# A state-space vision block on one core: the first pair of images is scanned by rows first, and half of its projections are made in slots beside the scans

## The chip, the core and the metric

The kernel runs as one program on one core of one Trainium2 chip. A core has five engines that run beside each other and meet at semaphores: PE (matrix products), DVE (vector work), ACT (functions of one operand), POOL (a second, slower vector engine) and SP, which here does nothing but issue DMAs, one after the other. The metric is the device time of one launch in microseconds (us). Instructions of one engine start in the order in which the program lists them; an instruction that waits holds up everything behind it on its engine. For SP that means that one DMA that waits for its data holds up all later DMAs.

## What is computed

Eight images of 96 channels and 64 x 64 pixels go through three layers: a state-space block with a convolutional branch, linear attention, and a feed-forward layer in reduced precision. The change bears on the first of them. Cut to what matters:

```python
def ss2d(x, ...):                                  # x: (8, 64, 64, 96), normalized
    xi, z = split(einsum('bhwc,oc->bhwo', x, in_proj_w), 2)
    xi = silu(conv2d(xi, conv_w, conv_b, groups=192))          # depthwise 3x3
    x_flat = xi.reshape(b, 192, L)                             # rows,    L = 4096
    x_wh   = transpose(xi, (0, 1, 3, 2)).reshape(b, 192, L)    # columns
    xs = [x_flat, x_wh, flip(x_flat), flip(x_wh)]              # k = 0, 1, 2, 3
    dts, Bs, Cs = split(einsum('bkdl,kcd->bkcl', xs, x_proj_w), [6, 22])
    dts = einsum('bkrl,kdr->bkdl', dts, dt_w)
    for each step l:                                           # 192 channels x 16 states
        h = exp(softplus(dts + bias) * A) * h + delta * u * B
        y = sum_n h * C                                        # plus D * u
    y = out_y[0] + flip(out_y[2]) + turned(out_y[1]) + turned(flip(out_y[3]))
    return einsum('bhwd,cd->bhwc', layer_norm(y) * silu(z), out_proj_w)

x1  = x * skip_scale + ss2d(layer_norm(x))
cb  = conv2d(gelu(conv2d(layer_norm(x1), w1)), w2)             # then channel attention
out = x1 * skip_scale2 + cb * sigmoid(...)
```

Each image is scanned four times: along its rows forwards (k = 0) and backwards (k = 2), and along its columns forwards (k = 1) and backwards (k = 3).

## The kernel before

**Pairs and scans.** The eight images are taken in four pairs p. The 192 channels of two images make three tiles T of 128 partitions: image 0's first 128 channels, image 1's first 128, and the last 64 of both. For each pair there are four sweeps k. A sweep runs over four chunks of 1024 steps (ci) and the three tiles, which is 12 jobs, and a job over 16 units of 8 channels x 16 states; so a sweep has 192 units and the kernel 3072. For one unit PE spreads delta * u over the states (`pu`, function spread), DVE multiplies by B (`pb`) and scans (`hc`, function scan), POOL multiplies by C, and PE adds the states up (`yp`, function total). ACT makes the decays (`da`). The sweeps come in the order (1, 3, 0, 2) for each pair, so columns first. A later sweep adds to what an earlier one of the same kind left: k = 3 to k = 1 (`prev`), k = 2 to k = 0 (`prev`) and, through `yet`, to the columns' sum.

**Slots and lanes.** All other work of phase_b is written as Python generators, called lanes, and handed out while the program is written. There are two slots to a pair of units, so 16 to a job and 3072 to the scans. In each slot every lane may put down its next few instructions. A lane that needs PSUM calls `take`, which gives out one of two banks (`pg`, `yp`) if the budget for PE and ACT isn't used up; the budget grows by RATE (1.4 for PE, 1.6 for ACT) with each slot. Nothing is decided at run time: the order on each engine is fixed when the program is built (class InOrder ties it down).

**The lanes.** before_scans(p) makes what pair p's scans need: norms (layer norm, stored in a padded image ua_d), convs (nine-tap convolutions on PE with weights wmain and wmix, the gate z with wz, then silu, and the projection of the rows), turn (POOL turns rows into columns) and at last the projection of the columns. It starts at the beginning of pair p-1's sweeps and works on one image after the other. columns(p) adds the two column sweeps, turned back, to D * u. It is put in during the k = 0 sweep of the same pair. after_scans(p) runs gate (layer norm, silu gate, output projection) and then starts two lanes rest (the convolutional branch, attention and feed-forward) for pair p during pair p+1. For the last pair, last_gate and last_rest do a part of this at the end, and a tail after the scans does what is left.

**The first pair.** No scans lie in front of it. So phase_a makes its whole first stage before the scans: for each of the two images one load of 1.5 MB, statistics on DVE (L108, L110), normalization on DVE (xn, L136 and L137) and on POOL (xt, L138 and L139), transposes (L145, L157), then eight blocks of two nine-tap convolutions and one gate product (L184, L193), POOL copies to columns (L203, L206), stores, and 8 row and 8 column projections (L221, L222, L225, stored by L227). The convolution weights are multiplied together on DVE from taps loaded one by one (projections, L64 to L66).

After phase_a come the loads of phase_b's weights (function load, L403), the feed-forward weights' casts, and zeros for the borders of the padded images: a zeroed tile is written over ua_d, u_d and g_d in 18 DMAs (L479). Then SP issues the first job's loads: `st` and `du`, `bm` (B for 32 x 4 rows), the store and reload of delta (`dl`), `cm`.

```python
        jobs = [
            (p, k, ci, T) for p in range(NP) for k in (1, 3, 0, 2)
            for ci in range(NCH) for T in (0, 2, 1)
        ]
```

Of the kernel before, what the change touches and what calls it, by code (L numbers as in the profile page):

```python
# [71 lines left out]
def phase_a(tc, a, proj, xi_d, zs_d, inp_d, xd_d):  # L72
# [3 lines left out]
    wmain, wmix, wz, xwa, xwb, convb = proj  # L76
    with ExitStack() as ctx:
        cp = ctx.enter_context(tc.tile_pool(name="a_const", bufs=1))
        xp = ctx.enter_context(tc.tile_pool(name="a_x", bufs=2))
        sp = ctx.enter_context(tc.tile_pool(name="a_small", bufs=2))  # L80
        op = ctx.enter_context(tc.tile_pool(name="a_out", bufs=2))
        bp = ctx.enter_context(tc.tile_pool(name="a_big", bufs=1))
        ps = ctx.enter_context(tc.tile_pool(name="a_ps", bufs=6, space=PSUM))
        pst = ctx.enter_context(tc.tile_pool(name="a_pst", bufs=1, space=PSUM))

        ident = cp.tile([128, 128], F32, name="ident")
# [3 lines left out]
        vec = cp.tile([C, 10], F32, name="vec")  # L90
        nc.sync.dma_start(vec, a["vec96"])
# [3 lines left out]
        for i in range(2):  # L95
            pad = cp.tile([C, H + 2, W + 2], F32, name=f"pad{i}")
            nc.gpsimd.memset(pad, 0.0)
            pads.append(pad)

        for b in range(2):  # L100
            p, half = divmod(b, 2)
            xt = xp.tile([128, G, C], F32, name="xt")
            nc.sync.dma_start(xt, a["x"][b].rearrange("(g p c) -> p g c", p=128, c=C))

            st = sp.tile([128, G, 6], F32, name="st")
            tmv = sp.tile([128, G, 2], F32, name="tmv")
            for g in range(G):
                nc.vector.bn_stats(st[:, g, :], xt[:, g, :])  # L108
            for g in range(G):
                nc.vector.bn_aggr(tmv[:, g, :], st[:, g, :])  # L110
            tm, tv = tmv[:, :, 0], tmv[:, :, 1]
            gps = pst.tile([128, 2, G], F32, name="gps")
            nc.tensor.matmul(gps[:, 0, :], mean128, tm, start=True, stop=True)
            gm = sp.tile([128, G], F32, name="gm")
            nc.vector.tensor_copy(gm, gps[:, 0, :])
            q = sp.tile([128, G], F32, name="q")
# [3 lines left out]
            nc.tensor.matmul(gps[:, 1, :], mean128, q, start=True, stop=True)  # L120
            r = sp.tile([128, G], F32, name="r")
            nc.scalar.activation(r, gps[:, 1, :], AF.Sqrt, bias=eps)
            nc.vector.reciprocal(r, r)

            s = sp.tile([128, G], F32, name="s")
# [6 lines left out]
            def wide(v):  # L132
                return v.unsqueeze(2).to_broadcast([128, G, C])

            xn = xp.tile([128, G, C], F32, name="xn")
# [3 lines left out]
            nc.gpsimd.tensor_mul(xt, xt, wide(r))  # L139

            pad = pads[b % 2]
            for j in range(8):
                tp = ps.tile([128, 512], F32, name="ps")
                for g in range(4):
                    nc.tensor.transpose(  # L145
                        tp[0:C, g * 128 : g * 128 + 128], xn[:, 4 * j + g, :], ident
                    )
                nc.scalar.activation(
                    pad[:, 1 + 8 * j : 9 + 8 * j, 1 : W + 1],
                    tp[0:C, :].rearrange("p (h w) -> p h w", w=W),  # L150
                    AF.Identity,
                    bias=vec[:, LN1B : LN1B + 1],
                    scale=vec[:, LN1G : LN1G + 1],
                )
                ti = ps.tile([128, 512], F32, name="ps")
                for g in range(4):
                    nc.tensor.transpose(  # L157
                        ti[0:C, g * 128 : g * 128 + 128], xt[:, 4 * j + g, :], ident
                    )
                if j % 4 == 0:  # L160
                    inp = op.tile([C, 2048], F32, name="inp")
                nc.vector.tensor_copy(inp[:, (j % 4) * 512 : (j % 4) * 512 + 512], ti[0:C, :])
                if j % 4 == 3:
                    nc.sync.dma_start(inp_d[b][:, (j - 3) * 512 : (j + 1) * 512], inp)


            rows = slice(64 * half, 64 * half + 64)
            xis = bp.tile([128, L], F32, name="xis")
            mix = bp.tile([128, L], F32, name="mix")
            xiw = bp.tile([128, L], F32, name="xiw")  # L170
            mixw = bp.tile([64, L], F32, name="mixw")

            def flipped(t, at):
                return t.rearrange("p (w h) -> p h w", h=H)[:, at.start // W : at.stop // W, :]

            for j in range(8):
                if j % 4 == 0:
                    zss = op.tile([128, 2048], F32, name="zss")
                at = slice(j * 512, j * 512 + 512)
# [20 lines left out]
                nc.scalar.activation(zss[:, (j % 4) * 512 : (j % 4) * 512 + 512], pz, AF.Silu)  # L200
                if j % 4 == 3:
                    cols = slice((j - 3) * 512, (j + 1) * 512)
                    nc.gpsimd.tensor_copy(  # L203
                        flipped(xiw, cols), xis[:, cols].rearrange("p (h w) -> p h w", w=W)
                    )
                    nc.gpsimd.tensor_copy(  # L206
                        flipped(mixw, cols), mix[0:64, cols].rearrange("p (h w) -> p h w", w=W)
                    )
                    nc.sync.dma_start(xi_d[0][p][half][:, cols], xis[:, cols])
                    nc.sync.dma_start(xi_d[0][p][2][rows, cols], mix[0:64, cols])  # L210
                    nc.sync.dma_start(zs_d[p][half][:, cols], zss)
                    nc.sync.dma_start(zs_d[p][2][rows, cols], mix[64:128, cols])
            nc.sync.dma_start(xi_d[1][p][half], xiw)
            nc.sync.dma_start(xi_d[1][p][2][rows, :], mixw)
            for o, main, rest in ((0, xis, mix), (1, xiw, mixw)):
                for j in range(8):
                    if j % 2 == 0:
                        xd = op.tile([PR, 1024], F32, name="xd")
                    at = slice(j * 512, j * 512 + 512)
                    px = ps.tile([128, 512], F32, name="ps")  # L220
                    nc.tensor.matmul(px[0:PR, :], xwa[:, o, :], main[:, at], start=True, stop=False)  # L221
                    nc.tensor.matmul(  # L222
                        px[0:PR, :], xwb[0:64, o, :], rest[0:64, at], start=False, stop=True
                    )
                    nc.vector.tensor_copy(xd[:, (j % 2) * 512 : (j % 2) * 512 + 512], px[0:PR, :])  # L225
                    if j % 2 == 1:
                        nc.sync.dma_start(xd_d[o][b][:, (j - 1) * 512 : (j + 1) * 512], xd)  # L227
# [88 lines left out]
def wait(n):  # L316
    for _ in range(n):
        yield
# [63 lines left out]

def phase_b(
    tc, a, proj, xi_d, xd_d, dl_d, ya_d, ys_d, y_d, zs_d, inp_d, x1_d, ua_d, u_d, g_d, cb_d, tn_d,
# [7 lines left out]
    with ExitStack() as ctx:  # L392
        cp = ctx.enter_context(tc.tile_pool(name="b_const", bufs=1))
        inner = ExitStack()
        bcp = inner.enter_context(tc.tile_pool(name="b_bc", bufs=4))
        wp = inner.enter_context(tc.tile_pool(name="b_w", bufs=2))
        hp = inner.enter_context(tc.tile_pool(name="b_h", bufs=8))
        gp = inner.enter_context(tc.tile_pool(name="b_bg", bufs=1))
        psc = inner.enter_context(tc.tile_pool(name="b_ps", bufs=1, space=PSUM))
# [6 lines left out]
        def unit(i):  # L406

            return gp.tile([128, 8 * PH if i in (0, 1, 6, 7) else 512], F32, name=f"u{i}")
# [20 lines left out]
        wmain, wmix, wz, xwa, xwb, convb = proj  # L429
# [27 lines left out]
        w1f, w2f = unit(0)[0:C, 0:HID], unit(1)[:, 0 : 3 * C]  # L457
        nc.sync.dma_start(w1f, a["w1T"])
        nc.sync.dma_start(w2f, a["w2T"].rearrange("p i c -> p (i c)"))
        b1r = load("b1", [128, 3])  # L460
        nc.vector.tensor_copy(w1q, w1f, saturate=False)
        nc.vector.tensor_copy(w2q.rearrange("p i c -> p (i c)"), w2f, saturate=False)
        nc.vector.tensor_copy(b1q, b1r, saturate=False)
        nc.vector.tensor_copy(b2q, vec[:, B2 : B2 + 1], saturate=False)
        nc.vector.tensor_copy(b1f, b1q)
        nc.vector.tensor_copy(b2f, b2q)
# [6 lines left out]
        zeros = gp.tile([128, 2048], F32, name="big0")  # L473
        nc.gpsimd.memset(zeros, 0.0)
        for i in range(2):
            for t, n in ((ua_d[i], C), (u_d[i], C), (g_d[i], 32)):
                for c0 in range(0, PH * PH, 2048):
                    c1 = min(c0 + 2048, PH * PH)
                    nc.sync.dma_start(t[:, c0:c1], zeros[0:n, 0 : c1 - c0])  # L479
# [13 lines left out]
            (p, k, ci, T) for p in range(NP) for k in (1, 3, 0, 2)  # L493
# [4 lines left out]
        turned = set()  # L498
# [52 lines left out]
        def columns(p):  # L551

            yield from slots.take_big(0, 1)
# [1320 lines left out]
```

## Time and profile before

| | |
|---|---|
| runs of the kernel | 11,445.26 us median of 3 (11,439.81 to 11,451.60) |
| the profiled execution: its own time, its span | 11,441.71 us, 11,439.9 us |
| mean granted PE clock | 0.814 of full speed |
| busy: DVE, POOL, PE, ACT | 92%, 79%, 71%, 57% of the span |
| DMA | 1,818 MB, mean 159 GB/s, one hardware queue |
| one unit: pb, hc on DVE | 1.216 us, 2.27 to 2.33 us |
| one unit: hc on POOL | 2.358 us |

The profile is of one execution. Busy time of an engine is the sum of its instructions; idle time costs only where the engine is the bound. A row names the tile that an instruction writes and those that it reads, as in "hc<-hc,cm". Line L242 is the helper through which all of phase_b's ordered instructions go, so there rows are told apart by tiles and not by lines. The chain of waits follows the last instruction back to what released it, and so on to the start; "issue" in it is time in which nothing that the profile shows was waited for. The windows give each engine's busy time in a stretch, and the granted clock there.

### The profile page before, as it was taken

Reading aid. Unit: us, or ns where it says so; the run is one execution under the profiler, and the core shown is the slowest. Engines: PE = TensorE matmul, PEld = TensorE weight load, DVE = VectorE, ACT = ScalarE, POOL = GpSimd, SP = SyncE. Lnnn points to the kernel's source line nnn. Section 1 sums busy time; section 2 is a strip of 40 time slices with the busy share of each in tenths; the row PEclk is TensorE's granted clock in tenths of the full one; section 3 lists DMA queues with packets and bytes.
Section 4 is the critical chain, followed back from the end, with each engine's and each line's share of the span. In section 5 each row is a group of like instructions: output and inputs, shape, how many; then the busy total and the mean of one; then the engine's idle time right before and its main releaser. Section 6 shows DMA issues by size and latency. Waiting matters only on the chain.

```text
span 11439.9 us, 127234 instructions
## 1 busy us (share of the span) xinstructions
PE 8086.3 (71%) x39524; PEld 3206.6 (28%) x39524; DVE 10551.6 (92%) x6613; ACT 6548.1 (57%) x9092; POOL 8995.2 (79%) x6573
## 2 busy tenths in 40 slices
PE   7658677465577876687767887677757677665778
PEld 3223222122222332233222333233322233222223
DVE  2399999999999999899999999999999999999984
ACT  1265555444466666666556666666646656774554
POOL 1387778977788779978889778987979889997870
PEclk9778778677788887788878888788878887777889
DMA  2444445554455555645545556644645555553551
GB/s 67 145 128 151 145 142 175 176 179 142 141 159 159 158 177 186 198 151 183 187 149 165 155 164 187 199 158 154 212 146 166 160 164 189 178 170 126 173 159 37
DMA packets 876693, 1818.33 MB, mean 159 GB/s; under 512 B 234669, under 2 KB 413614, under 8 KB 867246
## 3 DMA queue, kind: packets, MB, share of 16 engines
q1 hardware_dynamic: 876014, 1810.20, 50.4%
q8 instruction: 313, 5.13, 0.2%
q14 instruction: 366, 3.00, 0.1%
HBM read 1389.34 MB, written 420.42 MB: 158 GB/s over the span
## 4 chain that ended last, share of the span: by engine, by line
PE 38%; issue 26%; DVE 17%; POOL 7%; ACT 6%; DMA 4%; SPq 1%; DVEq 0%; POOLq 0%; ACTq 0%
PE pu L242 13%; PE yp L242 13%; DVE hc L242 10%; PE pg L242 8%; DVE pb L242 6%; POOL hc L242 5%; ACT u L242 2%; PE ps L184 2%; ACT da L242 2%; PE t L242 2%; DMA bm<-xd 1%; POOL u L242 1%; ACT L242 1%; DMA xd<-xd 0%; POOL turn L242 0%
## 5 line engine op out<-in xcount | busy, mean ns | idle before, releaser
L242 POOL TENSOR_TENSOR hc<-hc,cm 128x1024 f32<-128x1024 f32 x3072 | 7226.8, 2358 | 754.3 <-DVE hc L242 516.1
L242 DVE TENSOR_TENSOR_SCAN hc<-da,carry,pb 128x1024 f32<-128x1024 f32 x2304 | 5272.2, 2330 | 61.7 <-ACT da L242 59.0
L242 PE MATMUL pu<-du,c_sel 128*128 128x512 f32 x3072 | 2477.0, 953 | 2282.1 <-DVE pb L242 2278.2
L242 DVE TENSOR_TENSOR pb<-pu,bm 128x1024 f32<-128x1024 f32 x3072 | 3595.4, 1216 | 237.4 <-PE pu L242 193.4
L242 ACT ACTIVATE da<-dl,c_alog 128x1024 f32<-128x1024 f32 x3072 | 3356.1, 1140 | 132.9 <-DVE hc L242 111.9
L242 ACT COPY y<-yp 128x256 f32<-128x256 f32 x768 | 284.1, 370 | 2828.0 <-PE yp L242 2728.9
L242 PEld LDWEIGHTS pu<-du,c_sel 128*128 128x128 f32 x3072 | 807.6, 287 | 3571.2 <-DVE pb L242 2793.3
L242 DVE TENSOR_TENSOR_SCAN hc<-da,pb 128x1024 f32<-128x1024 f32 x768 | 1710.8, 2269 | 44.4 <-ACT da L242 44.1
L242 PE MATMUL yp<-hc,c_add 128*32 128x256 f32 x24576 | 1645.3, 413 | 63.7 <-ACT dls L242 40.1
L242 PEld LDWEIGHTS yp<-hc,c_add 128*32 128x32 f32 x24576 | 765.5, 119 | 1218.4 <-issue 630.3
L242 POOL COPY carry<-hc 128x1 f32<-128x1 f32 x2304 | 422.0, 183 | 768.4 <-DVE hc L242 750.7
L242 ACT ACT_TABLE_LOAD x554 | 710.8, 1283 | 80.9 <-DMA du<-xi 54.3
L242 POOL TENSOR_TENSOR u<-u,u 96x512 f32<-96x512 f32 (+1 forms) x426 | 537.7, 1269 | 100.2 <-ACT u L242 95.8
L242 POOL TENSOR_TENSOR du<-du,dls 128x1024 f32<-128x1024 f32 x192 | 453.3, 2361 | 141.7 <-ACT dls L242 140.6
L242 ACT COPY u<-pg 128x512 f32<-128x512 f32 (+5 forms) x345 | 189.0, 548 | 454.9 <-PE pg L242 448.6
L242 PE MATMUL pg<-ain,wmain 96*128 96x512 f32 x864 | 422.2, 634 | 21.5 <-ACT u L242 19.4
L242 PE MATMUL pg<-ain,wmix 96*128 96x512 f32 x864 | 402.2, 609 | 30.0 <-ACT u L242 30.0
L242 ACT COPY u<-yp 128x512 f32<-128x512 f32 (+4 forms) x351 | 188.2, 536 | 388.0 <-PE yp L242 361.9
L242 PE MATMUL yp<-prev,ident 128*128 128x256 f32 x768 | 311.0, 496 | 12.2 <-ACT dls L242 7.1
L242 PEld LDWEIGHTS yp<-prev,ident 128*128 128x128 f32 x768 | 213.4, 279 | 344.4 <-issue 273.9
L242 PE MATMUL pg<-st,dtw 12*128 12x512 f32 x384 | 220.3, 654 | 78.5 <-DMA dtw<-in_dtw 45.0
L242 PE MATMUL yp<-u,c_centres 128*128 128x512 f32 (+3 forms) x578 | 266.3, 647 | 8.1 <-ACT u L242 4.0
(335 smaller groups left out, 7061.9 us busy)
## 6 DMA issues: line engine op xcount, KB each, us to landing
dl<-dl SPq DMA_DIRECT2D x768, 512.0 KB
bm<-xd SPq DMA_DIRECT2D x512, 512.0 KB
cm<-xd SPq DMA_DIRECT2D x512, 512.0 KB
du<-xi SPq DMA_DIRECT2D x192, 512.0 KB
dl<-dls SPq DMA_DIRECT2D x192, 512.0 KB
ya<-y SPq DMA_DIRECT2D x384, 128.0 KB
prev<-ya SPq DMA_DIRECT2D x384, 128.0 KB
xi<-u SPq DMA_DIRECT2D x120, 256.0 KB
```

What stands on the lines that cost most here:

```text
L184: nc.tensor.matmul(pc.rearrange("p (h w) -> p h w", w=W), w[:, t, :], pad[:, 8 * j + dy : 8 * j + dy + 8, dx : dx + W], start=(t == 0), st ...
L242: op(*args, **kw)
```

## The change

1. Pair 0's sweeps come in the order (0, 2, 1, 3): rows first. The other pairs keep theirs.
2. phase_a loads and normalizes the two images in eight pieces of 7 to 9 groups of 128 pixels. Only the first half of each image is convolved there, in four chunks of 1024 pixels, with row projections and no column work. Both normalized images are written, padding included, to ua_d. It comes after the opening of phase_b's weight pool and ahead of the scans' pools, and calls projections itself after the first piece.
3. before_scans runs for p = 0 as well, from the first job: convolutions for j = 4 to 7 of both images, in two lanes at a time, then turn and the column projections, then fill. For p = 1 it starts when that has ended, also with two convs lanes, and two norms lanes. For p = 2 and 3 it is as it was.
4. fill is new: in slots it casts the feed-forward weights and writes the zeros of u_d and g_d. The zeros for ua_d go away.
5. columns(0) runs during pair 1, ahead of pair 0's gate. It reads the rows' result and adds it to the columns; pair 0's k = 2 sweep doesn't load `yet`.
6. A scan job's first loads are only put down once its data are there (the set `there`); if they aren't, 16 slots at a time are handed out with no scan in them.
7. RATE rises to 1.5 and 1.7. The last gate's start is tied to the slot at which a chunk is left, and not to a fixed number.

The diff, cut to its core:

```diff
@@ phase_a
+        pieces = [
+            (b, g0, g1) for at in (((0, 9), (9, 17)), ((17, 25), (25, 32)))
+            for b in range(2) for g0, g1 in at
+        ]
+        for b, g0, g1 in pieces:
+            xt = xp.tile([128, 9, C], F32, name="xt")
+            nc.sync.dma_start(
+                xt[:, 0 : g1 - g0, :],
+                a["x"][b].rearrange("(g p c) -> p g c", p=128, c=C)[:, g0:g1, :],
+            )
...
+        got = normalize(*pieces[0])
+        proj = wmain, wmix, wz, xwa, xwb, convb = projections(tc, a, pp)
+        for n, (b, g0, g1) in enumerate(pieces):
+            transposes(b, g0, g1, *got)
+            if n + 1 < len(pieces):
+                got = normalize(*pieces[n + 1])
+            if n < 4:
+                chunk(b, n % 2)
+            elif n % 2:
+                nc.sync.dma_start(ua_d[b], pads[b].rearrange("c h w -> c (h w)"))
@@ Slots
-    RATE, CAP = (1.4, 1.6), (2.2, 2.2)
+    RATE, CAP = (1.5, 1.7), (2.2, 2.2)
@@ phase_b
-        zeros = gp.tile([128, 2048], F32, name="big0")
-        nc.gpsimd.memset(zeros, 0.0)
-        for i in range(2):
-            for t, n in ((ua_d[i], C), (u_d[i], C), (g_d[i], 32)):
-                for c0 in range(0, PH * PH, 2048):
-                    c1 = min(c0 + 2048, PH * PH)
-                    nc.sync.dma_start(t[:, c0:c1], zeros[0:n, 0 : c1 - c0])
...
-            (p, k, ci, T) for p in range(NP) for k in (1, 3, 0, 2)
+            (p, k, ci, T) for p in range(NP) for k in ((1, 3, 0, 2) if p else (0, 2, 1, 3))
@@ columns
+            to = ys_d[0] if p else y_d
...
+                    if p == 0:
+                        yr = unit(c % 2)[:, 0:512]
+                        nc.sync.dma_start(yr, y_d[p][T][:, at])
...
+                    if yr is not None:
+                        ge.tensor_add(t, t, yr)
@@ after_scans
+            if p == 0:
+                yield from columns(p)
+            while resting:
+                yield
             yield from gate(p, range(8))
@@ new
+        def fill():
...
+            se.copy(w1q, w1f, saturate=False)
...
+            ge.memset(big, 0.0)
+            yield from wait(2)
+            for i in range(2):
+                for t, n in ((u_d[i], C), (g_d[i], 32)):
+                    for c0 in range(0, PH * PH, 2048):
+                        c1 = min(c0 + 2048, PH * PH)
+                        nc.sync.dma_start(t[:, c0:c1], big[0:n, 0 : c1 - c0])
+                        yield
@@ before_scans
+            js = range(0 if p else 4, 8)
+            at_once = p < 2
...
+            if at_once:
+                for half in range(2):
+                    slots.lanes.append(convs(2 * p + half))
+                    if p:
+                        slots.lanes.append(norms(2 * p + half))
+                while len(there_all) < 2:
+                    yield
...
+            there.update((p, 1, c) for c in range(NCH))
+            if p == 0:
+                yield from fill()
+                slots.lanes.append(before_scans(1))
@@ the loop over units
+                        if p == 0 and T == 0:
+                            slots.lanes.append(before_scans(0))
+                        if p > 0 and T == 2:
+                            slots.lanes.append(columns(p))
...
+                        while (p, k % 2, c) not in there:
+                            for _ in range(16):
+                                slots.run()
+                        slots.first = steps(job)
```

## The prediction

> **What bounds the kernel now.** I read the page's busy shares first (DVE 92%, no other engine over 79%), then the windows, to see where the other 8% of DVE lies, then the chain of waits there.
>
> Windows at the start; columns are the stretch, its length, busy time (instructions) of PE, weight loads, DVE, ACT and POOL, the granted clock, the DMA share and GB/s:
>
> ```profile
> core 0: us, PE busy (x) PEld busy (x) DVE busy (x) ACT busy (x) POOL busy (x), PEclk, DMA share, GB/s
> ...
> 100.00:200.00 100.00, 100.00 (x235) 43.98 (x234) 0.00 (x0) 11.83 (x18) 7.42 (x2) 1.00 0.10 32
> ...
> 400.00:500.00 100.00, 32.40 (x55) 8.79 (x58) 35.74 (x38) 20.35 (x20) 22.53 (x17) 0.58 0.70 218
> 500.00:600.00 100.00, 52.72 (x312) 20.05 (x304) 100.00 (x62) 52.20 (x92) 80.69 (x66) 0.72 0.38 117
> ```
>
> The front is PE-bound with DVE idle; from 500 us on DVE is full. The first scan starts at 475.81 us, the last ends near 11,100, and the tail takes 340 us. The front's chain, in order of time (start, length, what):
>
> ```profile
> 79.01 15.46 PE ps L184 x36
> ...
> 364.69 15.47 PE ps L184 x36
> 380.92 3.70 POOL mixw L206
> 386.14 14.01 DMA xd<-xd
> ...
> 430.36 2.11 SPq L479
> ...
> 462.95 6.29 DMA dl<-dls
> 471.06 5.82 DMA du<-xi
> ```
>
> To be seen: 16 blocks of two nine-tap convolutions, two strings of projections that wait for xd stores, then 26 us in which SP issues border zeros (L479, 427.8 to 454.3), then the load-up of the first scan.
>
> The scans, by sweep (192 units each): pair 0's four, then pair 1's third:
>
> ```profile
> 475.80:1129.60 653.80, 437.60 (x2092) 165.59 (x2092) 644.59 (x384) 368.14 (x564) 511.40 (x364) 0.78 0.44 138
> 1129.60:1799.40 669.80, 482.34 (x2260) 197.08 (x2260) 645.99 (x386) 375.38 (x576) 512.32 (x365) 0.80 0.48 149
> 1799.40:2457.30 657.90, 387.69 (x1950) 140.68 (x1950) 644.96 (x385) 313.57 (x355) 564.89 (x445) 0.75 0.54 180
> 2457.30:3101.50 644.20, 362.45 (x1983) 165.93 (x1982) 644.20 (x386) 269.81 (x292) 501.04 (x349) 0.76 0.45 146
> ...
> 4446.00:5140.30 694.30, 500.54 (x2391) 198.30 (x2391) 646.53 (x385) 444.58 (x653) 601.39 (x462) 0.81 0.55 175
> ```
>
> A sweep costs 644 us of DVE whatever lies beside it; the rest is stall: 9, 24, 13 and 0 us in pair 0 (46 together), 48 in the fullest sweep. So the time is front + 16 x 645 + stalls + tail. The change cuts the front and moves its work into slots; the order of k within pair 0 leaves the scans' DVE work as it is.
>
> **The front, part by part.** The changed kernel's own issue order was read for what comes before the first scan on each engine.
>
> *Convolutions and projections.* A block (18+18 matmuls and wz's two) repeats every 16.31 us (79.01 to 95.32). Eight of 16 stay: 130.5 us, so 130.5 go. A projection is 2.02 us (L221 and L222); 32 become 8: 16 us stay, 48 go, and the waits for xd stores (14 us at 386) with them.
>
> *Border zeros and weights.* 26 us of SP issue leave the chain: ua's zeros are dropped (whole padded images are stored instead), u_d's and g_d's move into slots behind the columns. The L403 loads, issued between 390 and 427, move beside the first transposes.
>
> *Earlier start.* The input comes in pieces of 7 to 9 of 32 groups. Whole, it took 8.42 us; 9/32 is 2.4 us and it now leads the queue, so say it is there at 5. Statistics 9 x (0.163+0.069) = 2.1; serial steps: two PE 1.3, two ACT 0.6, twelve small DVE operations of 0.2, two passes over the piece at 3.36 x 9/32 = 0.95, 1.9 of the next piece's statistics between them. DVE also stands still beside POOL (a 0.2 us multiply, L126, took 8.99 us while POOL ran L97 and L138): four passes of 5.33 x 9/32 = 1.5 make 6. First transposes at 21, against 61.6.
>
> *Sum.* The taps load in pairs, two buffers, each behind DVE, so the first block ends about 42. Seven blocks 114; projections 16; transposes of pieces two to four 5 (0.44 us for four); hand-offs between pieces 10 (estimate): 187. Pieces five to eight: transposes 7, a serial normalization 8, the pad's write 1: 203. Here the change adds a wait: in SP's order the first bm load stands behind ua's second store (1.67 MB, 8 to 9 us at 218 GB/s), which must land; behind it are the other bm loads, the dl store and the dl loads, and the first scan waits for all of them. 212. Four bm issues 3, then as before from dl store to scan (462.95 to 475.81) 13, and 8 to 10 for SP, where many rows wait for a store eight rows earlier (estimate): **first scan at 238** (215 to 270), a gain of 238.
>
> **What the slots take on.**
>
> *Half images in the first sweep*: eight j, over slots 1 to 92 of the first 192. The nearest row is the same work now (eight j of the second pair, "pg<-ain"), between two stretches of other lane work:
>
> ```profile
> 640.00:878.00 238.00, 138.56 (x733) 50.77 (x732) 238.00 (x143) 141.90 (x253) 196.44 (x157) 0.73 0.43 132
> 878.00:1160.00 282.00, 237.19 (x1025) 93.32 (x1025) 272.80 (x162) 153.66 (x178) 206.26 (x120) 0.89 0.44 144
> ```
>
> It costs DVE 9 us in 282. The Trainium skill speaks against such a move: "TensorE: Matmul & The Clock Gate" (Part 1, What's actually happening) says the array's clock is halved by default and freed only by sustained activity, and slots break up PE's work. Priced so, eight j are 2 x 130.5 = 261 us, beside 138.56/238 x 282 = 164 of other PE work: 425 in 282, a stall of 143. But the row shows 0.89 granted there, against 0.73 in the stretch before: the convolutions themselves keep the clock up. I take 10; the page's 143 is the upper end.
>
> *Columns*: 48 POOL copies of 0.62 us and 16 projections (2.02 us of PE each), in slots 102 to 205, where little else runs and POOL now is busy 511 of 654: a few us, inside the next figure. Without that cover it would be their 62 us.
>
> *Pair 1's first stage* starts at slot 232 instead of 16, with norms and convs of both images at once: 16 j of each in 244 slots (about 805 us), where it had 384. PE: 16 x 18.3 us = 293, at clock 0.89 329, and the scans' own 362.45/644.2 x 805 x 0.76/0.89 = 387: 716 of 805, 89%, against 237/282 = 84% in the row above, so stalls of about 5%, 40 us. Pair 0 in all: 10 + 40 + 15 at the edges = 65 against 46: **+20** (bounds 0 and +140). Two loads and a matmul fewer there (yet, 48 x 2 x 0.4 us of PE) are inside.
>
> *columns(0) moves into pair 1*, ahead of its gate: 48 POOL additions of 0.854 and 24 of about 1.27, 24 multiplies on ACT of 0.72: 71 and 17 us. Pair 1's idle slots at its end take the time; its fullest sweep has POOL at 601 of 694. **+10** (0 to 25).
>
> *Budgets 1.4/1.6 become 1.5/1.7*: 7% more lane work per slot in all pairs, ending earlier. Pairs 1 and 2 stall about 114 each (sweep lengths less DVE busy): 7% of it is about **+8** (-5 to +25).
>
> *Queues in the first sweep*: counted as the planner hands them out, slots are the same number in both kernels. Half-image chunks are finished in slots 50 and 93 and asked for in 80 and 128; columns in 205, asked for in 368: no scan waits for an empty slot. The zeros' 12 stores pass SP one a slot; SP has 3.3 us a slot.
>
> *Tail*: same code, same trigger slots. Nothing.
>
> Sum: -238 + 20 + 10 + 8 = **-200**, on the execution's own 11,441.7: 11,242; the runs' median (11,445.3) is 3.6 higher: **11,245**.
>
> **Rivals.**
>
> - *The front starves* (0.14): PE waits for taps, inp buffers (two, each freed by a store that SP issues late) and in-order SP, as it waits on xd stores now (14.01 us). Against it: loads come first in the queue. At 80 us of waits, 11,325.
> - *Lanes are free* (0.11): the front comes to 220 and the freed clock (0.89) absorbs the rest; for it, sweep four's zero stall. 11,205.
> - *PE becomes the bound* (0.04), slower than before: 24 j of convolutions lie in pair 0's first two sweeps; at half clock each spills into DVE. It decides from 11 us of stall a j (24 x 11 = 264, less the 46 there now, makes up the 220 otherwise gained); at 15 us 11,540. For: PE is the releaser of most DVE idle. Against: 1.2 us a j in the row above.
> - *The change doesn't do what it says* (0.02): data wouldn't be there and 16 empty slots of 3.3 us be inserted; one such batch is 53 us, 11,300. The slot counts speak against it.
>
> **How the numbers follow.** The forecast holds 0.69, its own range 11,215 to 11,290. The range to 11,200 and 11,330 takes in the free lanes and most of the starved front. What can be told from no change is 0.2%, 23 us: faster 0.95 (all but the bound PE and little of the rest), within 0.01, slower 0.04.
>
> **What would show it.** First scan near 238; PE at clock 1.0 in 45 to 185 with few gaps; between PE's last transpose and the first scan some 35 us, with the ua store in the chain; pair 0's first sweep some 655 to 660 long, its second the longest of the four; pair 1 some 10 longer. Wrong if the first scan is past 280, or pair 0's sweeps together exceed 2,700.

## The result, and the profile after

The changed kernel takes **11,307.9 us** (median of 4 runs, 11,304.6 to 11,312.9) against 11,445.8 for the kernel before beside it: a ratio of **0.988, 95% interval 0.9863 to 0.9897**, 138 us less. The forecast was 11,245. The profiled execution took 11,307.0 us, with a span of 11,305.2.

The page of the changed kernel, its first part (busy us, share of the span, instructions):

```profile
span 11305.2 us, 127593 instructions
...
PE 8037.9 (71%) x39452; PEld 3168.4 (28%) x39452; DVE 10538.6 (93%) x6651; ACT 6622.9 (59%) x9183; POOL 9032.5 (80%) x6649
```

DVE's work is what it was (10,552 before). Its share rose from 92% to 93%, as the span lost 135 us and the work did not.

Next, the chain of waits of the changed kernel up to its first scan (start us, length us, what):

```profile
43.02 15.45 PE ps L188 x36
...
160.86 15.45 PE ps L188 x36
...
203.50 0.68 ACT pad L161
204.18 11.45 issue
215.63 2.04 PE pg L245 x2
217.67 1.72 PE yp L245 x2
219.41 0.70 ACT dls L245
220.13 7.33 DMA dl<-dls
```

PE works on convolutions, transposes and projections until 181 (137 of the 140 us from 45 to 185, at a granted clock of 1.00), and the last half image is normalized serially to 204. Then comes 11.45 us of "issue", in which the chain shows no cause. SP's queue shows one (start us, length us, what):

```profile
204.19 0.30 SPq L229 DMA_DIRECT2D ua<-pad  x1
207.00 2.70 SPq L176 DMA_DIRECT2D inp<-inp  x2
209.79 1.96 SPq L1218 DMA_DIRECT2D ain<-ua  x1
213.79 0.60 SPq L1351 DMA_DIRECT2D bm<-xd  x1
```

SP's waits between 180 and 240 us (line waited for, us in total, times, longest) say what held the last of these:

```profile
SPq L1351 <- DMA ua<-pad: 1.9, 1, 1.9
```

ua's second store is issued at 204.19, and bm, which the first scan needs, only at 213.79. In between SP issues two more stores and a load; the wait that ends last, 1.9 us, is for ua's store to land. That is the added wait of the prediction. The first scan starts at 233.7 (475.8 before).

The windows of the changed kernel over pair 0's four sweeps; columns as in the prediction (busy us and instructions of PE, weight loads, DVE, ACT, POOL; granted clock; DMA share; GB/s):

```profile
233.70:902.70 669.00, 451.42 (x2131) 169.47 (x2132) 645.39 (x384) 331.76 (x374) 527.21 (x396) 0.82 0.48 159
902.70:1606.40 703.70, 525.91 (x2405) 217.71 (x2405) 647.03 (x385) 428.42 (x753) 520.59 (x376) 0.82 0.50 155
1606.40:2285.10 678.70, 477.22 (x2186) 176.62 (x2186) 646.41 (x386) 353.66 (x444) 532.73 (x404) 0.80 0.50 164
2285.10:2929.00 643.90, 333.71 (x1870) 141.09 (x1870) 643.90 (x386) 270.24 (x287) 501.17 (x349) 0.73 0.41 135
```

A sweep still costs DVE 644 to 647. Length less DVE busy is the stall: 24, 57, 32 and 0 us, 113 in the pair where the prediction had 65. The whole balance; each pair counts from its first scan to the first scan of the next, pair 3 to the end of the last scan:

| part | before | after | difference | predicted |
|---|---|---|---|---|
| to the first scan | 475.8 | 233.7 | -242 | -238 |
| pair 0 | 2,625.7 | 2,695.3 | +70 | +20 |
| pair 1 | 2,697.7 | 2,733.2 | +35 | +10 |
| pair 2 | 2,702.3 | 2,702.0 | 0 | } |
| pair 3 | 2,597.8 | 2,604.7 | +7 | } +8 for the budgets, over all pairs |
| tail after the last scan | 340.7 | 336.3 | -4 | 0 |
| span | 11,439.9 | 11,305.2 | -135 | -200 |

The front came as forecast. What is missing lies in the slots of pairs 0 and 1: 105 us given back instead of some 35.

What a stall there looks like, in the timeline of the changed kernel at the start of pair 0's second sweep (start us, length us, what; in brackets the idle time before it and its releaser). First PE, then ACT, then DVE:

```profile
1185.57 2.84 PE L245 MATMUL pg<-ain,wmain 96*128 96x512 f32 x6
...
1191.75 4.23 PE L245 MATMUL pg<-ain,wmix 96*128 96x512 f32 x6 [1.56 <-ACT u L245]
...
1196.98 1.88 PE L245 MATMUL pu<-du,c_sel 128*128 128x512 f32 x4
```

```profile
1188.45 0.59 ACT L245 COPY u<-pg 128x512 f32<-128x512 f32 x1 [2.19 <-PE pg L245]
1188.93 2.19 ACT L245 ACTIVATE da<-dl,c_alog 128x1024 f32<-128x1024 f32 x2
1191.02 0.67 ACT L245 ACTIVATE u<-pg,eps 96x512 f32<-96x512 f32 x1
```

```profile
1190.17 4.58 DVE L245 TENSOR_TENSOR_SCAN hc<-da,carry,pb 128x1024 f32<-128x1024 f32 x2 [2.53 <-ACT da L245]
1198.90 2.36 DVE L245 TENSOR_TENSOR pb<-pu,bm 128x1024 f32<-128x1024 f32 x2 [4.14 <-PE pu L245]
```

ACT's copy of a convolution waits 2.19 us for PE. `da` is next in ACT's order and comes after it, so the scan waits 2.53. A little later PE, which itself waited 1.56 for ACT to read a bank (`u<-pg,eps`), makes `pu` behind six more convolution matmuls and two of the norms, and DVE waits 4.14. Two in-order engines hand a delay to each other, and DVE pays 6.7 us in one place.

### The profile page after: what moved, and what is told of

It reads as the page before. It is cut to its first block, busy times and chain, and to the rows that moved or that the text cites. A ratio compares the mean times of both kernels' runs of the same rounds, so it can differ in the third digit from the quotient of the medians.

```text
span 11305.2 us, 127593 instructions
## 1 busy us (share of the span) xinstructions
PE 8037.9 (71%) x39452; PEld 3168.4 (28%) x39452; DVE 10538.6 (93%) x6651; ACT 6622.9 (59%) x9183; POOL 9032.5 (80%) x6649
## 4 chain that ended last, share of the span: by engine, by line
PE 39%; issue 24%; DVE 16%; POOL 8%; ACT 8%; DMA 4%; SPq 0%; DVEq 0%; POOLq 0%; ACTq 0%
PE yp L245 13%; PE pu L245 13%; PE pg L245 10%; DVE hc L245 9%; DVE pb L245 5%; POOL hc L245 5%; ACT u L245 3%; ACT da L245 3%; PE t L245 2%; ACT L245 1%; POOL u L245 1%; DMA bm<-xd 1%; POOL turn L245 1%; PE ps L188 1%; DMA cm<-xd 1%
## 5 line engine op out<-in xcount | busy, mean ns | idle before, releaser
L245 PE MATMUL pu<-du,c_sel 128*128 128x512 f32 x3072 | 2438.3, 939 | 2205.5 <-DVE pb L245 2201.9
L245 ACT COPY u<-pg 128x512 f32<-128x512 f32 (+5 forms) x384 | 212.8, 554 | 501.1 <-PE pg L245 490.2
L245 ACT COPY u<-yp 96x512 f32<-96x512 f32 (+5 forms) x336 | 179.9, 536 | 427.2 <-PE yp L245 409.1
L245 PE MATMUL pg<-ain,wmain 96*128 96x512 f32 x792 | 378.2, 622 | 30.3 <-ACT u L245 25.6
L245 PE MATMUL pg<-ain,wmix 96*128 96x512 f32 x792 | 370.9, 613 | 15.4 <-ACT u L245 15.0
L245 PE MATMUL yp<-prev,ident 128*128 128x256 f32 x768 | 308.1, 492 | 10.5 <-ACT dls L245 9.0
```

What stands on the lines that cost most here:

```text
L245: op(*args, **kw)
```

## The experiments

The theories, by the letters that the expectations use: **A**, both half images of pair 1 at once (first stage) overfill pair 0; **B**, the same work gives the same stall however it is ordered; **C**, the larger budgets cost time in all pairs; **D**, SP stands still where columns(0) loads y back; **E**, the gate is pushed back into the convolutions; **F**, the gate falls in step with pair 3's norms; **G**, ACT's budget is the one that binds; **H**, two convolution lanes get in each other's way. All times below:

| kernel | time | ratio to before, 95% interval | pair 0 | pair 1 | pair 2 | pair 3 |
|---|---|---|---|---|---|---|
| changed (1.5/1.7) | 11,307.9 | 0.988 (0.9863 to 0.9897) | 2,695 | 2,733 | 2,702 | 2,605 |
| e1_serial1 | 11,267.4 | 0.9846 (0.9832 to 0.9861) | 2,648 | 2,735 | 2,706 | 2,605 |
| e2_rate (1.4/1.6) | 11,194.9 | 0.9782 (0.9766 to 0.9798) | 2,659 | 2,702 | 2,663 | 2,599 |
| e3_yr4 | 11,314.6 | 0.9885 (0.987 to 0.99) | 2,696 | 2,733 | 2,706 | 2,605 |
| e4_nocol | 11,288.4 | 0.9865 (0.985 to 0.9879) | 2,693 | 2,704 | 2,706 | 2,605 |
| e5_delay | 11,300.4 | 0.9877 (0.9863 to 0.9892) | 2,696 | 2,727 | 2,694 | 2,606 |
| e6_before15 (before, 1.5/1.7) | 11,462.3 | 1.0018 (1.0011 to 1.0025) | 2,628 | 2,708 | 2,707 | 2,605 |
| e7_rate_serial1 | **11,178.1** | 0.9769 (0.9755 to 0.9784) | 2,647 | 2,700 | 2,662 | 2,599 |
| e8_rate13 (1.3/1.5) | 11,221.0 | 0.9808 (0.9791 to 0.9824) | 2,666 | 2,695 | 2,690 | 2,598 |
| e9_pe15 (1.5/1.6) | 11,221.4 | 0.9808 (0.9794 to 0.9823) | 2,673 | 2,711 | 2,671 | 2,597 |
| e10_act17 (1.4/1.7) | 11,316.8 | 0.9892 (0.9875 to 0.9908) | 2,698 | 2,728 | 2,705 | 2,605 |
| e11_rate145 (1.45/1.65) | 11,280.8 | 0.9859 (0.9844 to 0.9874) | 2,687 | 2,729 | 2,692 | 2,602 |
| e12_rate_token | 11,213.2 | 0.98 (0.9785 to 0.9815) | 2,680 | 2,695 | 2,667 | 2,597 |

The first scan lies between 232.8 and 236.6 in all but e6, so these are differences in the slots. The kernel before was run again beside each round and took 11,445.8, 11,442.2, 11,442.3 and 11,440.3, so differences of a few us between rows of different rounds say nothing.

### One image after the other

```diff
-            at_once = p < 2
+            at_once = p < 1
```

> Pair 1's first stage one image after the other again, in pair 0's slots 102 to 741, still before the scans that need it (752). Theory A (norms and convolutions of two images at once make the stall of pair 0's second and third sweep, 59 + 34 us): these two fall to about 25 + 25, time 11,308 - 45 = 11,265. Rival B (the same work costs the same stall wherever it lies): the stall only moves to other sweeps of pair 0, 11,300 to 11,315. Rival C (the higher budgets): within 8 us of 11,308.

Pair 0 fell by 47 us and the others stayed: A holds for the kernel as changed, and B falls. The second and third sweep took 660 and 665 us instead of 704 and 679; the fourth took 655, where it had stalled nowhere (644). What this costs with other budgets is in e7.

### The old budgets

```diff
-    RATE, CAP = (1.5, 1.7), (2.2, 2.2)
+    RATE, CAP = (1.4, 1.6), (2.2, 2.2)
```

> Budgets back to 1.4 and 1.6, nothing else. Theory C (the higher budgets pack lanes too densely): pairs 0 and 1 lose 25 to 40 us of stall, 11,275 to 11,285. Theory A and B: within 10 us of 11,308, since the lanes do the same work a little later.

113 us less than the changed kernel, where the prediction priced the budgets at 8. None of the theories had forecast so much; C came nearest, with 25 to 40. Pair 0 lost 36, pair 1 31, pair 2 39, pair 3 5. Pair 0's second and third sweep, windows of this kernel:

```profile
899.20:1583.20 684.00, 510.31 (x2385) 211.40 (x2384) 646.46 (x386) 418.26 (x732) 520.30 (x375) 0.82 0.52 159
1583.20:2249.10 665.90, 465.62 (x2186) 176.36 (x2186) 645.79 (x386) 357.66 (x459) 532.39 (x403) 0.81 0.51 163
```

DVE's busy time and the clock are those of the changed kernel within 1 us and 0.01, and PE's and ACT's within about 3%. The stalls went from 57 and 32 to 38 and 20. DVE's waits between 240 and 10,960 us (line waited for, us in total, times, longest), first of the changed kernel, then of this one:

```profile
DVE pb L245 <- PE pu L245: 233.6, 112, 7.8
DVE hc L245 <- ACT da L245: 133.5, 90, 5.4
```

```profile
DVE pb L245 <- PE pu L245: 176.7, 103, 6.4
DVE hc L245 <- ACT da L245: 94.9, 73, 5.1
```

Both waits shrink, together by 95.5 us, most of the 113. They are fewer and on average shorter (1.7 us against 2.1 for `pu`). What stands in front of `pu` when it is late is counted below, with ACT's budget alone.

### What columns(0) costs in pair 1

```diff
-                        yr = unit(c % 2)[:, 0:512]
+                        yr = unit(c % 4)[:, 0:512]
```

> columns(0) loads the rows' result into four tiles in turn instead of two. Theory D (SP stands at that load until POOL frees the tile, and bm loads behind it are late): the 7 to 10 us that DVE waits for bm in pair 1's first sweep go, 11,298. If SP only stands elsewhere (tile turn has two buffers too): 11,308 within 5.

```diff
-                yield from columns(p)
+                yield from slots.take_big(0, 1)
+                yield from wait(86)
+                slots.big.clear()
+                turned.add(p)
```

> columns(0) is left out, its 86 slots stay empty of it; pair 0's outputs lack the column sweeps. If columns(0)'s own instructions cost (theory D): pair 1's first sweep falls from 706 to about 690 (its jobs 2 and 3), time 11,290. If its cost is that it pushes the gate back by 104 slots into convs of pair 2 (theory E), the later jobs of that sweep keep their stall and the time falls by no more than 17; if all of the 36 us by which pair 1 grew goes, E is wrong: 11,272.

e4 leaves columns(0) out, so pair 0's result lacks the column sweeps; its 86 slots are kept. Without columns(0), pair 1's first sweep went from 706.0 to 676.8, and the whole kernel gained 20 us; the rest of the 29 is lost again in small differences of the front, pair 2 and the tail. DVE's waits in that sweep, first of the changed kernel, then of e4:

```profile
DVE pb L245 <- PE pu L245: 29.4, 12, 3.9
DVE hc L245 <- ACT da L245: 18.7, 11, 4.4
DVE pb L245 <- DMA bm<-xd: 10.5, 5, 6.1
```

```profile
DVE pb L245 <- PE pu L245: 20.7, 9, 3.7
DVE hc L245 <- ACT da L245: 10.5, 6, 2.8
```

The waits for bm are gone (10.5 us), and those for PE and ACT are 9 and 8 shorter. The first part is SP's. Its own waits in the changed kernel between 3,035 and 3,150 us (L624 is the store of a turned chunk, L610 the load of `big`):

```profile
SPq L624 <- POOL carry L245: 40.4, 6, 10.3
SPq L624 <- POOL turn L245: 18.0, 2, 9.3
SPq L610 <- POOL turn L245: 9.0, 1, 9.0
```

SP stands up to 10.3 us for the chunk that POOL has yet to finish (POOL's last instruction before it is another, `carry`), and loads for the scans stand behind it. DVE's longest wait for bm, 6.08 us at 3,094.75, follows the third row: SP stood from 3,072.9 to 3,082.0 for a tile of `big` that POOL still read, then 1.2 us for a store, and issued bm from 3,085.05 on. D looked for this wait at the load of `yr` and its two tiles; it is at the stores and at the load of `big`, and four tiles for `yr` left it: the three rows read 34.7, 20.2 and 9.3 us in e3_yr4, its sweep lost 7 us and the next gained 7, and the time did not fall (D had 11,298). So SP's wait in columns(0) is there, but in another place than D had it, and what DVE waits for it is about a third of the 29 us. E explains little: e4 holds the gate back by the same slots, and still took 29 of the 35 us by which pair 1 had grown.

### The gate later

```diff
             while resting:
                 yield
+            if p == 1:
+                yield from wait(17)
```

> The changed kernel with budgets 1.5 and 1.7 kept; only pair 1's gate starts 17 slots later, as it happened to do under 1.4 and 1.6. Theory F (with the lower budgets pair 2 got 39 us shorter because the gate no longer runs in step with pair 3's norms): pair 2 falls from 2,702 to about 2,665, pairs 0 and 1 stay, time 11,270. Theory C (the budgets' size): pair 2 stays at 2,702 and the time at 11,308, within 8.

Pair 2 went from 2,702 to 2,694, where F asked for most of the 39 us that the old budgets take from it, and the time by 7.5, little more than the kernel before differs between rounds (5.5). The gate's place alone is not the cause.

### The budgets alone, on the kernel before

```diff
-    RATE, CAP = (1.4, 1.6), (2.2, 2.2)
+    RATE, CAP = (1.5, 1.7), (2.2, 2.2)
```

> The kernel before with budgets 1.5 and 1.7 and nothing else. Theory C: its pairs 1 and 2 get 30 to 40 us longer each, 11,510. Theory F: where lanes meet in the same slots as before (gate and norms at 794 and 1562 in both), nothing changes much, 11,445 within 15.

20 us more (interval 13 to 29), within the prediction's bounds (+8, -5 to +25), and almost nothing in pair 0 (2,626 to 2,628). C had asked for 11,510, F for 11,445 within 15; neither came. The 113 us are therefore not the price of the budgets by themselves, but of these budgets on the changed schedule.

### Old budgets and one image after the other

The edits of e1 and e2 together.

> Old budgets and pair 1's first stage one image after the other. If both gains are their own: pair 0 from 2,659 to about 2,635, time 11,170. If the budgets already took what the serial stage takes (pair 0 was 2,695, 2,648 and 2,659): 11,185 to 11,195.

The fastest kernel of the study: 11,178.1, which is 130 us below the changed kernel and 264 below the kernel before beside it. With the old budgets the serial order takes 12 us from pair 0, not 47: the two costs overlap in large part.

### How the time follows the budgets

Only RATE differs: 1.3/1.5, then PE's alone (1.5/1.6), then ACT's alone (1.4/1.7), then halfway (1.45/1.65).

> Budgets 1.3 and 1.5 in the changed kernel. Theory C: stall falls on, by another 20 to 60 us, 11,150. Theory F: no trend, only other meetings of lanes, 11,150 to 11,230 either way, with pair 2 moving apart from the others.

> Budgets 1.5 for PE, 1.6 for ACT. With it the lanes of pairs 1 to 3 lie in the same slots as with 1.4 and 1.6. Theory G (the ACT budget is the one that binds, and its 1.7 makes the loss): 11,195 within 15. Theory C in its other form (PE over-filled): 11,260 or more.

> Budgets 1.4 for PE, 1.7 for ACT. Theory G: as the changed kernel, 11,290 to 11,310. PE over-filled: 11,210 or less.

> Budgets half way, 1.45 and 1.65; the gate starts with pair 3's norms as with 1.5 and 1.7. A loss that grows with the budgets gives about 11,250; a loss that belongs to particular meetings of lanes may give anything from 11,190 to 11,310, pair by pair without order.

ACT's budget alone gives the whole loss (11,317, against 11,308 with both), PE's alone a quarter of it (11,221, +27). DVE's waits in the kernel with ACT's budget alone, same stretch as above:

```profile
DVE pb L245 <- PE pu L245: 242.6, 112, 7.7
DVE hc L245 <- ACT da L245: 126.4, 90, 5.6
```

The wait that grew most, by 66 us over the old budgets, is for PE, though only ACT was given more. The kernel's text says how the two hang together: `take` gives out a bank only while both budgets are above zero (`min(self.left) > 0`), so where ACT's is the one used up, a larger one also lets more of PE's lane matmuls into a slot. The traces say what this does. `pu` has one buffer and can be made again once the last `pb` has read it. Where DVE then waited for `pu`, the time from the end of that `pb` to the start of `pu` was added up, and what PE did in it (us; counted from the traces, waits above 0.2 us, between the first scan and the last):

| kernel | `pu` late by, in all | lane matmuls in front of it | PE waiting for ACT | number of DVE's waits |
|---|---|---|---|---|
| before | 326 | 280 | 35 | 76 |
| e6_before15 | 390 | 326 | 47 | 94 |
| e8_rate13 (1.3/1.5) | 378 | 305 | 39 | 92 |
| e2_rate (1.4/1.6) | 374 | 295 | 47 | 100 |
| e9_pe15 (1.5/1.6) | 387 | 305 | 48 | 102 |
| e11_rate145 (1.45/1.65) | 422 | 330 | 67 | 101 |
| e10_act17 (1.4/1.7) | 484 | 387 | 67 | 110 |
| changed (1.5/1.7) | 482 | 393 | 63 | 110 |

Of the 110 us by which `pu` is later with ACT's budget raised, 93 are lane matmuls of PE that stand in front of it and 21 are PE waiting for ACT. So the delay is for the most part more filler work ahead of the due instruction, and to a smaller part the two engines waiting for each other. The first column puts the six budgets on the changed schedule in the same order as their times do, from 374 (11,195) to 484 (11,317).

G holds for the level, though both times lie a little outside what it asked (11,221 for 11,195 within 15; 11,317 for 11,290 to 11,310). The curve is not a straight line: 11,221, 11,195, 11,281, 11,308 from 1.3 to 1.5 on PE. From 1.4/1.6, a first step of 0.05 on both costs 86 us and the next 27, and a step of 0.1 down costs 26, where C had asked for a gain. A loss that grows evenly would have given about 11,250 halfway. A steady price per unit of budget would not do this. That it also counts which lanes meet in which slots is the likely reason; no run shows it directly.

### Turns for the two convolution lanes

On top of e2, the two lanes of pair 0's first sweep take their blocks in turn:

```diff
+                    while p == 0 and half != whose[0]:
+                        yield
                     x, nxt = nxt, None
...
                     yield from project(0, b, main, mix, slice(0, 64), ats[j], t)
+                    whose[0] = 1 - half
...
-            there_all = set()
+            there_all, whose = set(), [0]
```

> Old budgets, and in the first sweep the two convolution lanes take turns, one block of one image at a time. Theory H (two lanes in each other's way make the first sweep's 21 us of stall, against 9 in the row that I took): its length falls from 666 to about 655, time 11,185. If it is what eight j among fresh scans cost: 663 to 668, 11,195.

The first sweep did not move (665.1 against 665.6), so H falls. The second and third grew from 684.0 and 665.9 to 692.0 and 678.5. With turns, pair 1's first image load comes 112 us later (1,053.8 instead of 942.0) and its last 43 us later, so its first stage begins later and is pressed into fewer slots; that this is what costs the 21 us was not tested.

## Why the prediction was right, and where its sum was wrong

**In short.** The mechanism was right: the front shrinks, DVE's work stays, and part of the gain is paid back as stall in the slots. The size was within the wider range and outside the forecast's own (11,215 to 11,290). The part of the wider range that it fell into was meant for a starved front, which did not come. That it fell there at all is partly luck: two errors of opposite sign met, a budget term about 105 us too small, and a gain of some 40 us that was not forecast.

**What bounds it: right.** 16 sweeps of 645 us of DVE stayed. The change moved the front and the stalls alone.

**The front: right** (-238, measured -242). First transposes at 23 (21 forecast), first block's end at 43 (42), last chunk's projections at 181 (187), PE's last transpose at 204 (203), bm's wait for the ua store in its place (213.8, forecast 212), first scan at 233.7 (238), 30 us after the last transpose (35). The two estimates in it, hand-offs and SP's load-up, were a few us too large. The store was put at 8 to 9 us; 1.67 MB at 218 GB/s are 7.7, and bm was issued 9.6 after it.

**Half images in the first sweep: right in mechanism, too small.** The stall of the sweep is 24 us, not 10; of it 22 us lie in its first 306, which hold the convolutions (window of the changed kernel, columns as above):

```profile
233.70:540.00 306.30, 254.00 (x1077) 100.45 (x1077) 284.53 (x170) 166.53 (x193) 222.99 (x175) 0.90 0.41 135
```

The granted clock is 0.90 there and 0.73 in the sweep without convolutions. So the row was the better guide than the price that the prediction drew from the Trainium skill ("TensorE: Matmul & The Clock Gate", Part 1, What's actually happening), by which the stall came to 143 us. What failed in that price is not the page's rule that activity lifts the throttle, but the reading that slots break up PE's work enough to keep the clock halved: 0.90 is much nearer to the full clock.

**Pair 1's first stage in pair 0 (40 us): about right with the old budgets, too small with the new.** Pair 0's second and third sweeps stall 58 us in e2 and 89 in the changed kernel, where the sum had some 55 with the edges. In all, pair 0 grew by 34 with the old budgets (predicted 20) and by 70 with the new. The term was worked out from PE's load (89%), whatever the order. e1 and e7 show that the order counts: the same work one image after the other takes 47 us less with the new budgets and 12 less with the old. (Its 805 us for 244 slots should be 820, at 645 us for 192; the load hardly changes.)

**columns(0) in pair 1 (+10, 0 to 25): too small at the high budgets, within its bounds.** Its first sweep gives 29 us, of which 20 show in the time; with the old budgets pair 1 as a whole grew by 4.

**The budgets (+8, -5 to +25): this term failed.** It was worked out as 7% of the stalls of pairs 1 and 2, that is, as a share of what the kernel before lost. The sum itself slipped: 7% of about 114 us is 8 for each pair, so 16 for both. On the kernel before, that is near the truth (+20). On the changed kernel they cost 113 us, and ACT's alone 122. The stalls from which it was scaled belonged to another schedule; the budgets act on the load that the change itself brings, so this term could not be added to the others as if it stood alone.

**The rest of the gap has the other sign.** With the old budgets the span is 246 us below the kernel before (11,194.1 against 11,439.9), 38 better than the 208 that the terms without the budgets add up to. As much, 39 us, is gained in pair 2 (2,702 to 2,663), which the prediction left alone. This is not settled: the same lanes took between 2,662 and 2,707 us in pair 2 over these kernels, and neither the gate's place (e5, 8 us) nor the budgets on the kernel before (5 us) gives it alone.

**The rivals.** The front did not starve, and the lanes were not free: pair 0's stall rose from 46 to 113. PE did not become the bound; at 24 j in the first two sweeps, the 113 us of pair 0 are less than 5 us a j, short of the 11 from which that rival decides. Its price is partly there, though: of the signs named as making the forecast wrong, pair 0 above 2,700, it was 5 us short (2,695). The change did what it says. Of the sweeps, the second was the longest of the four, as said, but the first took 669, not 655 to 660, and pair 1 grew by 35, not 10.

## What to carry to other kernels

Price moved work at the budgets and in the slots that it will meet, not as a share of the stalls that stand in the profile: two edits that each load the same in-order engines do not add. Where a change moves work and retunes a budget at once, run the move with the old budget too. Here that alone is worth 113 us, nearly as much again as the whole change brought. Look at what a budget admits, too: one that is named for ACT can let in work for PE. And a budget that is tuned for one schedule has to be tried again after each move, in small steps, since its curve can have steps of 86 us.

## What was not expected of the hardware

- A larger ACT budget was paid for mostly in waits for PE (66 of 97 us of additional DVE waiting in e10 against e2). DVE's and ACT's busy times were the same (10,536.6 and 10,538.8; 6,606.0 and 6,606.3): the same work, in an order in which more of PE's lane matmuls stand in front of a due `pu` (387 us against 295).
- A store of 1.67 MB and a load behind it: from ua's second store (204.19) to the bm load (213.79) SP's queue took 9.6 us, and the last wait in it was for that store to land, with the first scan behind it.
- One store in SP's queue whose tile was not written yet held the loads behind it up to 10.3 us, and a load into a tile that POOL still read held them 9.0.
